# Row moves in two queues, routing in three steps, shared PSUM banks and earlier fetches in a four-layer gated network

## The chip, the cores and the metric

The kernel runs on one core of one Trainium2 chip, in one launch. The metric is the device time of one execution in microseconds (us); the number that counts is the median of several timed runs. One execution of each kernel is also recorded by the hardware profiler, and every duration of a single instruction comes from that record.

The engines are written as the profile writes them: PE is the matrix engine and PEld its weight loads, DVE the vector engine, ACT the scalar engine (activation functions and copies), POOL the GpSimd engine, SP the engine that issues most transfers. Each engine carries out its own instructions in the order in which they stand in its stream and waits for the others by semaphores. So an instruction that waits also holds up all that stand behind it on the same engine.

## What is computed

The input x has 32 sequences of 128 tokens with 128 features. Four layers follow, each with an attention part and a feed-forward part, both added to x through a learned gate tanh(g):

```
x = x + tanh(g_xattn[i]) * xattn_i(layernorm(x), ctx, ...)
x = x + tanh(g_ffn[i])   * ffn_i(layernorm(x))
```

- Layer 0: attention of 16 heads (width 8) to the context with a length mask; then a ternary-weight MLP of width 512.
- Layer 1: attention of 16 heads to the context and to x itself; then a block of its own: causal attention with rotary positions (16 heads of width 4), and a mixture of 8 experts of which each token takes its best 2 (width 256, SiLU gate).
- Layer 2: attention of 8 heads (width 16) to the context with a mask; then LayerNorm and a second mixture, best 2 of 8 experts (width 512, GELU).
- Layer 3: instead of attention a "depool": a decaying scan over the context, picked at boundaries that given lengths set, is added to a projection of x; then a feed-forward part whose weights are rounded to three values and whose activations are rounded to 8 bits per token (scale = 127 / max|x|).

The output is x after the fourth layer.

## The kernel before, in words

**Groups.** The 32 sequences are worked on in 8 groups of 4 (`NG`, `NB`). x stays on chip for the whole run, one tile per group (`xs[g]`).

**Attention.** `attention` cuts a group's heads into units of four and each unit into two halves. For a half it does three things: the maxima of the scores (products L476 on PE, `sc`, reduced by DVE at L507 or L512), which `placed` turns (L526) and writes into the stacked operand as extra rows by a transfer on SP (`mrows`); the weights (products `sct`, L476, then Exp on ACT, L542; L545 on POOL cuts off later tokens in the causal attention); and the products with the values (L559), whose result is copied (L565), turned (L571) and divided by its sum.

**The pipe.** `Pipe` sets the order in which the work is written down. One `turn` takes the maxima of one half, the weights of a half four turns back (`AHEAD`), and the products one turn after that. After each turn it carries out some of the row moves that are waiting (`move`), and one step of the first generator in `afters` (what follows a group's attention) and in `fill` (work put beside it: the MLP of layer 0; in layer 2 `last_layer`, which prepares the depool and the rounded weights of layer 3). `attend` runs it over all groups, the next group's `before` being advanced turn by turn; `drain` finishes what is left. A scheduler then places each engine's instructions; the order of the DMA moves on POOL is kept as written.

**Norms.** `layernorm` takes statistics on DVE (L211, L213) and leaves the power to -1/2 to POOL: `r` (L201), or, where two norms in a row are merged (`again`), `w` (L247); DVE waits for it and then scales (L234).

**Routing.** `Routes.take` gets the logits of a group (`pl`, L1052 in layer 1, L1216 in layer 2), takes softmax and the best two on DVE, and counts each expert's tokens by a product with a triangle (`pos`, L655 and L656), which gives each token a slot (`slot_r`, L662). It then queues 8 stores: each is an indirect DMA issued by POOL (L609) that writes 128 rows into the experts' rooms in DRAM. `Routes.run` goes through 23 blocks of 512 slots: it loads weights and rows (SP, L728 and L730), turns the rows (`transposed`, L265), and applies the expert (L1085 to L1090, or L1233 and L1236), the second product (`ye`, L746), and the way back (`yT`, L1094 or L1240, `yt`, L753). `fetch` then queues 8 indirect reads per group on POOL (L776), and `add` adds them with their weights on DVE (L788).

**The move queue.** Stores and fetches stand in one list, `to_move`. In layers 0 and 1 a turn issues 2 of them, in layer 2 4 of them; layer 2's `before(g)` empties the list before it adds, and queues the next group's fetch when it ends.

**PSUM.** Layer 2 has two accumulators for L559 (`av`), two tiles of two banks for scores, and two banks (`tp`) for all else. The expert loops have two banks for transposes, one for `ye`, four for the first products.

**Layer 3.** `depooled(g)` issues all queued moves, adds, takes the merged norm (w), queues the fetch of group g+1, and adds the projection and the depool, which layer 2 left in eight tiles on chip. `first(g)` takes the norm (r), issues the queued fetch, rounds (`quantized`: maximum L1254, then L1255, L1257, L1258, L1260 and the rounding L1263), and applies the gate and up weights (L1303, L1305, L1308). `second(g, h)` rounds again and applies the last product (L1324). The loop runs `depooled(g+2)`, `first(g+1)`, `second(g)`. The weights of this layer (`w3`) are loaded at L1064.

Of the kernel before, what the change touches and what calls it, by code (L numbers as in the profile page):

```python
# [25 lines left out]
SLOTS = 512  # L26
CAP = 4096
D = 128
EPS = 1e-5
MORE = (2 * CAP - E) // SLOTS  # L30
BLOCKS = E * CAP // SLOTS + MORE + 1
# [3 lines left out]
class _Cols:  # L35
# [15 lines left out]
    iota_p=1, rev=8, room=8,  # L51
# [10 lines left out]
W3 = _Cols(w_in=128, gate=512, up=512, down=512)  # L62


@with_exitstack
def tile_flamingo_gated(
# [316 lines left out]
    to_place, to_finish, to_move = [], [], []  # L383

    def move(n=None):
        for do in to_move[:n]:
            do()
        del to_move[:n]

    class Pipe:  # L390
# [6 lines left out]
        def __init__(self, moves):  # L397
            self.moves = moves
            self.todo, self.last, self.afters, self.place, self.fill = [], None, [], [[]], []

# [16 lines left out]

        def turn(self, ahead):
            self.place.append(to_place[:])
            to_place.clear()  # L420
            place = self.place.pop(0)
            ready = bool(self.afters)
            for do in to_finish + place:
                do()
            to_finish.clear()
            if len(self.todo) > ahead:
                self.todo[0][0]()
            if self.last:
                _, products, after = self.last
                products()  # L430
                if after:
                    self.afters.append(after())
            self.last = self.todo.pop(0) if len(self.todo) > ahead else None
            move(self.moves)
            if ready:
                self.advance(self.afters)
            self.advance(self.fill)

        def drain(self):
# [7 lines left out]
            move()  # L447
            while self.fill:
                self.advance(self.fill)
# [137 lines left out]
    class Routes:  # L587
# [3 lines left out]
        def __init__(self, keep, name):  # L591
            self.name = name
            self.slot = keep.tile([P, NG, 2, NB], I32, name=f"slot_{name}")
            self.weight = keep.tile([P, NG, 2, NB], F32, name=f"weight_{name}")
            self.total = keep.tile([P, E], BF, name=f"total_{name}")
            nc.vector.memset(self.total, 0.0)
            self.room = by_expert.pop()
# [17 lines left out]
        def take(self, pool, psum, g, logits, rows, gate, eps):  # L615

            def t(tag):
# [4 lines left out]

            tt = nc.vector.tensor_tensor
# [29 lines left out]
            tt(self.total, before[:, NB - 1], mine[:, NB - 1], ALU.add)  # L653
            pos = psum.tile([P, NB, E], F32, tag="tp", name="pos")
# [3 lines left out]
            tt(at, pos, CST(cst, "room")[:, None, :].to_broadcast([P, NB, E]), ALU.add)  # L658
# [4 lines left out]
            for b in range(NB):  # L663
                for k in range(2):
                    to_move.append(lambda b=b, k=k: self.store(rows[:, b, :], self.slot[:, g, k, b : b + 1]))
# [8 lines left out]
            )  # L674

        def tables(self, pool, psum):


            n = MORE
# [3 lines left out]
            nc.vector.tensor_scalar(nx, cnt, 1.0 / SLOTS, 0.5 - 0.5 / SLOTS, ALU.mult, ALU.add)  # L683
# [17 lines left out]
            nc.vector.tensor_scalar(row[:, 2], row[:, 0], float(CAP // SLOTS), 1.0, ALU.mult, ALU.add)  # L701
# [6 lines left out]
        def run(self, pool, psum, weights, cols, turned, hidden, n_f, finish):  # L708
# [3 lines left out]
            def static(i):  # L712
                return slice(i * (CAP // SLOTS), i * (CAP // SLOTS) + 1), slice(i, i + 1)

            def dynamic(i):
# [5 lines left out]
                    for k, top in ((1, BLOCKS - 1), (0, E - 1))  # L721
                ]
                return bass.ds(vals[0], 1), bass.ds(vals[1], 1)

            def load(i):
# [3 lines left out]
                xt = pool.tile([P, SLOTS // P, D], F32, tag="xt", name="xt", bufs=3)  # L729
# [5 lines left out]

            def first(i):
                block, w, xt = loaded.pop(i)
                xT = pool.tile([P, SLOTS], F32, tag="xT", name="xT")
                turned(xT, flat(transposed(psum, xt)))
                return block, w, hidden(w, xT)  # L740

            def second(block, w, hid):
                y = psum.tile([P, SLOTS], F32, tag="y", name="ye", bufs=1)
# [3 lines left out]
                yT = pool.tile([P, NB, P], F32, tag="yT", name="yT")  # L747
# [3 lines left out]
            def third(block, yT):  # L751
                yt = pool.tile([P, NB, D], F32, tag="yt", name="yt")
                nc.vector.tensor_copy(yt, transposed(psum, yT))  # L753
                ins = nc.sync.dma_start(out=self.room[block].rearrange("o p n -> (o p) n"), in_=flat(yt))
                self.apart(ins, "tiles", "no two tiles share a block")

            n = E + MORE
            loaded = {0: load(0), 1: load(1)}
            hid, done = first(0), None
            table = self.tables(pool, psum)  # L760
            for i in range(n):
# [6 lines left out]
                hid = after  # L768
            third(*done)

        def fetch(self, pool, g):

            got = pool.tile([P, 2, NB, D], F32, tag="got", name="got")
# [8 lines left out]
            to_move.extend(lambda b=b, k=k: one(b, k) for b in range(NB) for k in range(2))  # L782
            return got

        def add(self, g, got):
            for b in range(NB):
                for k in range(2):
                    nc.vector.scalar_tensor_tensor(  # L788
                        xs[g][:, b, :], got[:, k, b, :], self.weight[:, g, k, b : b + 1], xs[g][:, b, :],
# [14 lines left out]
    def attend(pipe, banks, jobs):  # L804


        layer, g = jobs[0]
        for _ in layer.before(g):
            pass
        for i, (layer, g) in enumerate(jobs):  # L810
            then, n = jobs[i + 1] if i + 1 < len(jobs) else (None, None)
# [4 lines left out]
        pipe.drain()  # L816

# [25 lines left out]

    by_expert = [dram.tile([BLOCKS, P, SLOTS // P * D], F32, name=f"by_expert{i}") for i in range(2)]
    clear = [(t, n) for t in by_expert[::-1] for n in range(0, BLOCKS, 4)]
    routes1 = Routes(cp, "r1")
    with ExitStack() as stack:
# [6 lines left out]
        class psum:  # L854


            @staticmethod
            def tile(shape, dtype, tag=None, name=None, bufs=None):
                return psum_h.tile(shape, dtype, tag="h", name=name)

        pipe = Pipe(2)
# [3 lines left out]
        def layer0():  # L865
# [5 lines left out]
            zeros = mlp.tile([P, SLOTS // P * D], F32, name="zeros")  # L871
            nc.gpsimd.memset(zeros, 0.0)
            def cleared():
                if clear:
                    t, n = clear.pop(0)
                    nc.sync.dma_start(
                        out=t[n : n + 4].rearrange("n p m -> p n m"),
                        in_=zeros[:, None, :].to_broadcast([P, 4, SLOTS // P * D]),
                    )
# [53 lines left out]
            def after(g):  # L933
                add_gated(xs[g], 0, at.pop(g)[-1])
                pipe.fill.append(mlp0(g))
                yield
# [5 lines left out]
        def layer1():  # L942
# [28 lines left out]
            def after(g):  # L971
# [13 lines left out]
                yield  # L985
# [3 lines left out]
        def layer1f():  # L989
# [42 lines left out]
            def after(g):  # L1032
# [20 lines left out]
                routes1.take(pool, psum, g, pl, t, 5, 0.0)  # L1053
                yield
# [10 lines left out]
    depool = [tail.tile([P, NB, D], F32, name=f"depool{g}") for g in range(NG)]  # L1065
# [4 lines left out]
    with ExitStack() as outer:  # L1070
# [3 lines left out]
        with ExitStack() as stack:  # L1074
# [5 lines left out]
            def swiglu(w, xT):  # L1080
                hid = pool.tile([P, 2, SLOTS], F32, tag="hid", name="hid", bufs=3)
                for f in range(2):
                    fs = slice(f * P, (f + 1) * P)
                    p1 = psum.tile([P, SLOTS], F32, tag="h", name="p1", bufs=4)
                    nc.tensor.matmul(p1, lhsT=E1(w, "w1")[:, fs], rhs=xT, start=True, stop=True)  # L1085
                    p3 = psum.tile([P, SLOTS], F32, tag="h", name="p3", bufs=4)
                    nc.tensor.matmul(p3, lhsT=E1(w, "w3")[:, fs], rhs=xT, start=True, stop=True)  # L1087
                    sil = pool.tile([P, SLOTS], F32, tag="sil", name="sil", bufs=3)
# [7 lines left out]
            routes1.run(pool, psum, e1_d, E1, turned, swiglu, 2, finish)  # L1096


        routes2 = Routes(cp, "r2")
        with ExitStack() as stack:  # L1100
            banks = attention_pools(stack, "a2", 2, 4)
            pool, psum, _, _ = banks
            pipe = Pipe(4)
# [3 lines left out]
            def last_layer():  # L1107
# [13 lines left out]
                for g in range(NG):  # L1121
# [43 lines left out]
                    nc.scalar.copy(depool[g], po)  # L1165
# [24 lines left out]
            def before(g):  # L1190
                if g == 0:
                    gots[0] = routes1.fetch(pool, 0)
                move()
# [10 lines left out]
            def after(g):  # L1204
# [14 lines left out]
                routes2.take(pool, psum, g, pl, yn, 6, 1e-8)  # L1219
                yield  # L1220
# [248 lines left out]
```

## Time and profile before

| | us |
|---|---|
| timed runs | 2245.47, 2238.03, 2245.99 |
| median of them | 2245.47 |
| the profiled execution | 2218.45 |
| its span, first to last instruction | 2216.7 |
| layers 0 and 1 with their attention (from the span's start) | 0 to 1250 |
| first expert loop | 1250 to 1420 |
| attention of layer 2 and its routing | 1420 to 1800 |
| second expert loop | 1800 to 2005 |
| layer 3 | 2005 to 2217 |

The profile's page gives for each engine its busy time, share of the span and number of instructions:

```profile
PE 1651.2 (74%) x13624; PEld 1005.0 (45%) x13624; DVE 1219.5 (55%) x3521; ACT 894.8 (40%) x1110; POOL 643.3 (29%) x645
```

In the same page the span is cut into 40 slices of 55.4 us. A digit is the busy share of a slice in tenths, and PEclk is the clock that PE was granted, in tenths of full speed:

```profile
PE   0699998989999998878777399545656449993444
DVE  7645455375545577676666333366677421113777
POOL 5101011010100113345554660254544310004440
PEclk9999999999999999877778599866677569996656
```

PE is nearly full through the first sixteen slices (layers 0 and 1) and again in slices 33 to 37 (the second expert loop). Between them, in layer 2 (slices 26 to 32), and after them, in layer 3, all engines have gaps. A line of a list of waits reads: engine and tile that waited, what it waited for, us in all, how many times, the longest. In a timeline a line is start, duration, engine, line of the code, operation, and in brackets the idle time before it and what ended it.

### The profile page before, as it was taken

Reading aid. Unit: us, or ns where it says so; the run is one execution under the profiler, and the core shown is the slowest. Engines: PE = TensorE matmul, PEld = TensorE weight load, DVE = VectorE, ACT = ScalarE, POOL = GpSimd, SP = SyncE. Lnnn points to the kernel's source line nnn. Section 1 sums busy time; section 2 is a strip of 40 time slices with the busy share of each in tenths; the row PEclk is TensorE's granted clock in tenths of the full one; section 3 lists DMA queues with packets and bytes.
Section 4 is the critical chain, followed back from the end, with each engine's and each line's share of the span. In section 5 each row is a group of like instructions: output and inputs, shape, how many; then the busy total and the mean of one; then the engine's idle time right before and its main releaser. Section 6 shows DMA issues by size and latency. Waiting matters only on the chain.

```text
span 2216.7 us, 35517 instructions
## 1 busy us (share of the span) xinstructions
PE 1651.2 (74%) x13624; PEld 1005.0 (45%) x13624; DVE 1219.5 (55%) x3521; ACT 894.8 (40%) x1110; POOL 643.3 (29%) x645
## 2 busy tenths in 40 slices
PE   0699998989999998878777399545656449993444
PEld 0454445456666666555455144233545324441222
DVE  7645455375545577676666333366677421113777
ACT  0376565556777654332333133211112114341334
POOL 5101011010100113345554660254544310004440
PEclk9999999999999999877778599866677569996656
DMA  6574567544232342112121254244344023331110
GB/s 213 147 244 164 181 204 274 162 116 121 86 99 89 99 118 67 51 54 58 51 60 34 79 167 149 94 115 127 99 119 109 21 84 124 118 116 38 29 36 22
DMA packets 162232, 240.46 MB, mean 108 GB/s; under 512 B 20304, under 2 KB 102032, under 8 KB 161808
## 3 DMA queue, kind: packets, MB, share of 16 engines
q1 hardware_dynamic: 153872, 221.42, 32.6%
q0 software_dynamic: 8192, 16.79, 2.7%
q8 instruction: 107, 1.75, 0.3%
q14 instruction: 61, 0.50, 0.1%
HBM read 137.64 MB, written 99.14 MB: 107 GB/s over the span
## 4 chain that ended last, share of the span: by engine, by line
PE 39%; DVE 14%; POOL 13%; issue 7%; ACT 3%; DMA 3%; SPq 0%; POOLq 0%; DVEq 0%; ACTq 0%
PE ye L746 5%; POOL got L776 5%; PE sct L476 4%; PE av L559 4%; POOL by_expert L609 4%; PE ph L1233 4%; PE sc L476 3%; PE ph L918 3%; PE tp L265 3%; DVE mx L507 2%; DMA got<-by_expert,slot_r 2%; PE p L1087 2%; PE p L1085 2%; DVE bst L211 1%; PE tpo L571 1%
## 5 line engine op out<-in xcount | busy, mean ns | idle before, releaser
L542 ACT ACTIVATE w<-sct 128x1024 f32<-128x1024 f32 x288 | 292.6, 1024 | 315.4 <-PE sct L476 312.8
L507 DVE TENSOR_REDUCE mx<-sc 128x8 f32<-128x1024 f32 x160 | 194.6, 1218 | 133.1 <-PE sc L476 132.5
L476 PEld LDWEIGHTS <-stack_q 96*128 96x128 bf16 x2560 | 189.0, 107 | 119.9 <-issue 96.1
L776 POOL DMA_INDIRECT got<-by_expert,slot_r x128 | 126.5, 989 | 354.9 <-issue 354.1
L559 PE MATMUL av<-w,va 128*9 128x128 f32 (+2 forms) x3584 | 200.4, 296 | 37.8 <-POOL w L545 31.7
L512 DVE TENSOR_REDUCE mx<-sc 128x4 f32<-128x1024 f32 x128 | 152.8, 1221 | 130.0 <-PE sc L476 129.5
L476 PE MATMUL sc<-stack_k,stack_q 96*128 96x128 bf16 x1536 | 141.7, 237 | 40.6 <-DVE mx L507 16.5
L476 PE MATMUL sct<-stack_q,stack_k 128*128 128x128 bf16 (+1 forms) x1536 | 140.0, 234 | 21.8 <-DVE mx L507 12.7
L476 PEld LDWEIGHTS <-stack_k 128*128 128x128 bf16 (+1 forms) x1536 | 109.5, 105 | 76.0 <-issue 72.7
L559 PEld LDWEIGHTS av<-w,va 128*9 128x9 f32 (+2 forms) x3584 | 100.2, 94 | 88.4 <-POOL w L545 42.3
L294 POOL CAST hml<-whole 128x512 bf16<-128x512 f32 (+1 forms) x56 | 36.7, 655 | 354.7 <-ACT whole L293 181.5
L746 PE MATMUL ye<-hid,w 128*128 128x512 f32 x276 | 133.3, 593 | 2.3 <-DVE hid L1090 2.3
L201 POOL TENSOR_TENSOR r<-r,m 128x4 f32<-128x4 f32 x56 | 57.1, 1020 | 230.9 <-DVE r L200 219.7
L918 PE MATMUL ph<-h,w 128*128 128x512 f32 x256 | 122.7, 606 | 1.8 <-ACT hn L921 0.9
L918 PE MATMUL ph<-hn,w 128*128 128x512 f32 x256 | 121.2, 604 | 0.7 <-ACT hn L921 0.7
L565 ACT COPY ot<-av 128x512 f32<-128x512 f32 x112 | 65.4, 584 | 128.9 <-PE av L559 90.7
L476 PE MATMUL sc<-stack_l,stack_q 96*128 96x128 bf16 x1024 | 109.8, 237 | 0.0
L1227 DVE TENSOR_SCALAR xT<-tp,col 128x512 f32<-128x512 f32 x23 | 18.6, 809 | 154.9 <-PE tp L265 137.5
L545 POOL TENSOR_SCALAR_AFFINE_SELECT w<-w 128x1024 f32<-128x1024 f32 x64 | 70.3, 1098 | 109.5 <-ACT w L542 109.4
L476 PE MATMUL sct<-stack_q,stack_l 128*128 128x128 bf16 x1024 | 98.8, 234 | 2.7 <-DVE mx L507 2.5
L542 ACT ACT_TABLE_LOAD x72 | 92.4, 1283 | 9.7 <-PE sct L476 8.5
L571 PE MATMUL tpo<-cst,ot 128*128 128x128 f32 x448 | 81.2, 305 | 13.7 <-ACT ot L565 6.6
(289 smaller groups left out, 3345.2 us busy)
## 6 DMA issues: line engine op xcount, KB each, us to landing
by_expert<-zeros SPq DMA_DIRECT2D x40, 1024.0 KB
stack_q<-q SPq DMA_DIRECT2D x96, 288.0 KB
stack_k<-k SPq DMA_DIRECT2D x96, 288.0 KB
k<-hml SPq DMA_DIRECT2D x16, 1152.0 KB
w<-in_e_dram SPq DMA_DIRECT2D x23, 514.5 KB
xt<-by_expert SPq DMA_DIRECT2D x46, 256.0 KB
by_expert<-yt SPq DMA_DIRECT2D x46, 256.0 KB
q<-hml SPq DMA_DIRECT2D x72, 128.0 KB
```

Of the source, the lines that this page charges most:

```text
L476: nc.tensor.matmul(dst[:, h * P : (h + 1) * P], lhsT=stat[rows, 4 * e + h, b], rhs=mov[rows, 4 * e + h, b], start=start and h == e == 0, s ...
L507: nc.vector.tensor_reduce(mx[:, :, b0 : b0 + 2].rearrange("p h b -> p b h"), sc.rearrange("p i (h k) -> p i h k", h=4), AX.X, ALU.max, neg ...
L512: nc.vector.tensor_reduce(mx[:, :, b0], sc.rearrange("p i (h k) -> p h i k", h=4), AX.XY, ALU.max, negate=True,)
L542: nc.scalar.activation(w.rearrange("p i h k -> p i (h k)"), sc, AF.Exp)
L545: nc.gpsimd.affine_select(out=heads, in_=heads, pattern=[[0, 8], [1, P]], compare_op=ALU.is_ge, fill=0.0, base=0, channel_multiplier=-1,)
L559: nc.tensor.matmul(av[32 * h : 32 * h + dv + 1, b * P : (b + 1) * P], lhsT=values[c][:, b, 4 * u + h, :], rhs=w[:, i, h, :], start=c == 0, ...
L571: nc.tensor.transpose(tp[:, b].rearrange("p s r -> p (s r)"), ot[:, b, :], ident)
L609: ins = nc.gpsimd.indirect_dma_start(out=self.rows(), out_offset=bass.IndirectOffsetOnAxis(ap=slots, axis=0), in_=rows, in_offset=None,)
L746: nc.tensor.matmul(y, lhsT=w2[:, f, :], rhs=hid[:, f, :], start=f == 0, stop=f == n_f - 1)
L776: ins = nc.gpsimd.indirect_dma_start(out=got[:, k, b, :], out_offset=None, in_=self.rows(), in_offset=bass.IndirectOffsetOnAxis(ap=self.sl ...
L918: nc.tensor.matmul(ph, lhsT=wt[:, c, f * P : (f + 1) * P], rhs=h[:, c, :], start=c == 0, stop=c == 3)
L1233: nc.tensor.matmul(ph, lhsT=E2(w, "w1")[:, f * P : (f + 1) * P], rhs=xT, start=True, stop=True)
```

## The change

Eight things are altered.

1. `to_move` becomes two lists. A turn issues up to 3 fetches and 2 stores in every layer. Layer 2's `before(g)` empties only the list of fetches; `drain` issues what is left of the stores after all `afters` are done, and steps the work beside it meanwhile.
2. `Routes.take` yields twice: after the counts on DVE, before `pos`; and after the weights, before it queues the stores. The stores are queued one step later than before.
3. Layer 2's attention has one accumulator, four banks for scores as before, and three banks that all else shares (`shared`).
4. The depool rows go to DRAM by SP and come back, group by group, in layer 3.
5. The expert loops have two banks for `ye` and three for the first products.
6. In layer 3, `fetch(g)` issues the loads of the depool and the 8 fetches at once. `depooled(g)` does this for g+1 and g+2 right after its norm; the fetched rows have three buffers.
7. `quantized` computes max(am, 1e-5)/127 and its reciprocal (before: maximum, reciprocal, times 127, reciprocal), and the two products `fg` become one instruction.
8. The experts' rooms, slots and blocks are computed from a table (`LOTS`), with the values that they had. A few `yield`s at the ends of `after` go.

The load L1064 of layer 3's weights is written at the same place; in the built order it stands far earlier, since the pool that it belongs to has become smaller.

```diff
+        def beside(self):
+            for i, (fill, rate) in enumerate(self.fills):
+                self.owed[i] += rate
+                while self.owed[i] >= 1:
+                    self.owed[i] -= 1
+                    self.advance(fill)
...
-            move(self.moves)
+            move(to_fetch, 3)
+            move(to_store, 2)
             if ready:
                 self.advance(self.afters)
-            self.advance(self.fill)
+            self.beside()
...
-        def drain(self):
+        def flush(self):
             while self.todo or self.last:
                 self.turn(0)
...
             while self.afters:
                 self.advance(self.afters)
-            move()
-            while self.fill:
-                self.advance(self.fill)
+                self.beside()
+
+        def drain(self):
+            self.flush()
+            move(to_store)
+            for fill, _ in self.fills:
+                while fill:
+                    self.advance(fill)
...
             tt(self.total, before[:, NB - 1], mine[:, NB - 1], ALU.add)
+            yield
             pos = psum.tile([P, NB, E], F32, tag="tp", name="pos")
...
-            for b in range(NB):
-                for k in range(2):
-                    to_move.append(lambda b=b, k=k: self.store(rows[:, b, :], self.slot[:, g, k, b : b + 1]))
...
+            yield
+            for b in range(NB):
+                for k in range(2):
+                    to_store.append(lambda b=b, k=k: self.store(rows[:, b, :], self.slot[:, g, k, b : b + 1]))
...
-                y = psum.tile([P, SLOTS], F32, tag="y", name="ye", bufs=1)
+                y = psum.tile([P, self.slots], F32, tag="y", name="ye")
...
+    def shared(pool):
+
+        class psum:
+            @staticmethod
+            def tile(shape, dtype, tag=None, name=None, bufs=None):
+                return pool.tile(shape, dtype, tag="h", name=name)
+
+        return psum
...
-    depool = [tail.tile([P, NB, D], F32, name=f"depool{g}") for g in range(NG)]
+    depool = [dram.tile([P, NB * D], F32, name=f"depool{g}") for g in range(NG)]
...
-                    p1 = psum.tile([P, SLOTS], F32, tag="h", name="p1", bufs=4)
+                    p1 = psum.tile([P, 512], F32, tag="h", name="p1", bufs=3)
...
-            banks = attention_pools(stack, "a2", 2, 4)
-            pool, psum, _, _ = banks
-            pipe = Pipe(4)
+            pool, psum_a, avs, _ = attention_pools(stack, "a2", 1, 4)
+            psum_h = stack.enter_context(tc.tile_pool(name="beside_ps", bufs=3, space=PSUM))
+            psum = shared(psum_h)
...
-                    nc.scalar.copy(depool[g], po)
+                    nc.scalar.copy(dep, po)
+                    nc.sync.dma_start(out=depool[g], in_=flat(dep))
...
-                move()
+                move(to_fetch)
                 routes1.add(g, gots.pop(g))
...
-                    ph = psum.tile([P, SLOTS], F32, tag="h", name="ph", bufs=4)
+                    ph = psum.tile([P, 512], F32, tag="h", name="ph", bufs=3)
...
-            nc.vector.tensor_scalar(am, am, 1e-5, None, ALU.max)
+            inv = pool.tile([P, NB], F32, tag=f"inv_{tag}", name=f"inv_{tag}")
+            nc.vector.tensor_scalar(inv, am, 1e-5, 1.0 / 127.0, ALU.max, ALU.mult)
             sc = pool.tile([P, NB], F32, tag="qs", name="qs")
-            nc.vector.reciprocal(sc, am)
-            nc.vector.tensor_scalar(sc, sc, 127.0, None, ALU.mult)
-            inv = pool.tile([P, NB], F32, tag=f"inv_{tag}", name=f"inv_{tag}")
-            nc.vector.reciprocal(inv, sc)
+            nc.vector.reciprocal(sc, inv)
...
+        def fetch(g):
+            if g < NG and g not in fetched:
+                dp = pool.tile([P, NB, D], F32, tag="dp", name="dp", bufs=3)
+                nc.sync.dma_start(out=flat(dp), in_=depool[g])
+                fetched[g] = routes2.fetch(pool, g, 3), dp
+                move(to_fetch)
+
         def depooled(g):
-            move()
-            routes2.add(g, fetched.pop(g))
+            got, dp = fetched[g]
+            routes2.add(g, got)
             _, h = layernorm(pool, xs[g], tag=None, again="hx")
-            if g + 1 < NG:
-                fetched[g + 1] = routes2.fetch(pool, g + 1)
+            fetch(g + 1)
+            fetch(g + 2)
...
             y = layernorm(pool, xs[g])
-            move()
             q, inv = quantized(y, D, "x")
...
+        fetch(0)
         depooled(0)
         depooled(1)
         h = first(0)
```

## The prediction, made before the changed kernel was run

> **What bounds the kernel now.** I read first the table of windows, one per stage: busy us, then the granted TensorE clock.
>
> ```profile
> 0.00:1250.00 1250.00, 1038.17 (x10218) 642.16 (x10218) 749.59 (x1959) 632.12 (x723) 317.69 (x356) 0.93 0.39 120
> 1250.00:1440.00 190.00, 147.73 (x463) 72.34 (x463) 63.89 (x109) 55.97 (x93) 72.05 (x35) 0.90 0.43 139
> 1440.00:1700.00 260.00, 149.47 (x1517) 116.87 (x1520) 173.27 (x670) 46.77 (x64) 133.33 (x141) 0.67 0.43 113
> 1700.00:1800.00 100.00, 41.11 (x415) 32.46 (x407) 48.84 (x223) 11.92 (x17) 35.97 (x35) 0.59 0.13 40
> 1800.00:2005.00 205.00, 188.51 (x559) 90.28 (x559) 36.56 (x59) 80.18 (x116) 0.00 (x0) 0.97 0.35 119
> 2005.00:2217.00 212.00, 86.26 (x460) 50.85 (x460) 147.38 (x504) 67.85 (x97) 84.22 (x80) 0.62 0.11 30
> ```
>
> The columns are PE, PEld, DVE, ACT, POOL, clock, DMA share, GB/s. Layers 0 and 1 (to 1250) and the two expert loops (to 1440, to 2005) are PE's. In layer 2 (1440 to 1800) and the last layer (from 2005) no engine is full: waits decide. So I read the waits there, then the timelines of DVE and POOL, and last the chain of one period. Layer 2's waits, 1440 to 1700, and the expert loops' (1290 to 1418, then 1810 to 1995):
>
> ```profile
> PE pos L655 <- DVE t_mine L648: 31.6, 4, 12.0
> DVE y L234 <- POOL r L201: 25.3, 8, 7.2
> DVE y L234 <- POOL w L247: 10.2, 5, 5.2
> ```
>
> ```profile
> PE tp L265 <- ACT yT L1094: 6.0, 21, 0.7
> ```
>
> ```profile
> PE tp L265 <- ACT yT L1240: 8.3, 21, 0.4
> ```
>
> PE stands in front of the routing's `pos` product 31.6 us, and DVE for the LayerNorms' powers on POOL 35.5 us. DVE's timeline in the tail of layer 2, the idle time before each in brackets:
>
> ```profile
> 1742.87 0.18 DVE L245 TENSOR_SCALAR w<-bmv 128x4 f32<-128x4 f32 x1
> 1751.12 1.12 DVE L234 TENSOR_SCALAR y<-x,bmv,w 128x128 f32<-128x128 f32 x4 [8.07 <-POOL w L247]
> ...
> 1767.69 0.16 DVE L245 TENSOR_SCALAR w<-bmv 128x4 f32<-128x4 f32 x1
> 1777.05 1.11 DVE L234 TENSOR_SCALAR y<-x,bmv,w 128x128 f32<-128x128 f32 x4 [9.20 <-POOL w L247]
> ```
>
> The power itself takes 1.67; the rest is eight stores (L609) queued ahead of it. The chain of one period of the last layer, 2091 to 2116:
>
> ```profile
> by line: POOL got L776 32.9%; DMA got<-by_expert,slot_r 20.5%; issue 11.7%; PE px L1279 7.3%; PE po L1324 5.5%; DVE bst L211 5.4%; POOL r L201 4.0%; DVE t L1329 2.8%; DVE h L1308 2.7%; PE tph L1319 2.6%; DVE x L273 2.6%; DVE bmv L213 2.3%;
> ...
> 2091.42 2.57 DMA got<-by_expert,slot_r
> ...
> 2103.78 1.01 POOL r L201
> 2104.96 1.01 POOL got L776
> ```
>
> There the chain runs through POOL's fetches and their landing.
>
> **The change part by part.** The base is the profiled execution, 2218.45 us (span 2216.7). A fetch or store holds POOL 0.95 with a 0.30 gap: eight take 10.0. Orders are those of the built changed kernel.
>
> *Causal attention of layer 1 (900 to 1240).* In five groups DVE waits for the first rotary add (L1020), 23.0 us in all: it starts at 1101.42 behind seven stores, inputs ready at 1095.7. Afterwards five stand there (six, then five, in one group): 2 x 1.25 x 5 = -12.5 at most. The two moved stores come later, one before the casts of the next parts. I take half: -6 (-11 to 0).
>
> *Layer 2 to 1700.* Three edits with one answer. Routing in pieces puts up to 27 score products and the transposes ahead of `pos` on PE in the first four groups: at most the 31.6 goes. But DVE (173 of 260 us) must still do each routing and the maxima. Three shared banks let transposes wait less for one another; only one accumulator bank stays, which the copy (L565, 0.58 us) must clear first: near nothing. The two queues put three instead of eight fetches ahead of the second group's stores (-5), but later powers stand behind up to seven stores and four fetches: +3 to +8 each where they are ready early. The depool rows now go to DRAM by SP, each behind an ACT copy; the stack loads behind it in SP's order can start about 3 us later (the first copy ends 1476.56, the next load went at 1473.33). In sum -25 to +20; of 31.6 gained and about 20 lost I take -8, nearer to the wait that is seen.
>
> *Tail of layer 2 (1700 to 1800).* Stores queue after all pieces of the groups, and only three of a group's own stand ahead of the next power instead of eight. Those powers were ready at 1717.1, 1743.05 and 1767.85 and ran at 1720.67, 1749.42 and 1775.34. The first keeps seven stores: -1.3. The second waits for 1739.5 + 3 x 1.25 = 1743.3, say 1743.5: -5.9. The third likewise 1769.3: -6.0. Behind each stands the path to the end: y, transpose, logits, routing, slot. The last group's 13 stores: five find the 11.8 us idle before 1788.77. -13 (-17 to -2; little if PE's or SP's work is late instead).
>
> *Expert loops.* A second bank for the second product lets the transpose of yT stand further from its copy: it waits 6.0 us in 128 and 8.3 us in 185. Over the loops at most -6 and -8. Three instead of four banks for the first products give some back: the fourth reuses a bank that a 0.8 us activation must free. Half: -7 (-14 to +5).
>
> *Weights of the last layer.* Their load (L1064, 0.85 MB) went ahead of the first expert's, whose rows landed 5.49 us after issue; it now goes far earlier: -2 (-3 to 0).
>
> *Last layer.* Now each power r follows w and then eight fetches; before it was w, r, fetches. Start: w0 ends 2020.61, sixteen fetches 20.0, w1 at 2040.8 (was 2033.76), eight fetches, r0 at 2052.7 (was 2037.14): +15.6. Steady: w to r becomes 1.67 + 0.2 + 10.0 = 11.9 (was 7.8, 2095.97 to 2103.78); r to w loses the waits for landing (0.24 + 1.33 + 0.76 = 2.3) and six small quantizer steps of about 0.1: 14.9 - 2.9 = 12.0. A period goes from 22.7 to 23.9: +1.2, four times. The last three groups have no fetch ahead of r and no landing to wait for: -2.3 each. 15.6 + 4.8 - 6.9 = +14 (+5 to +18). So what is late next, once the landings are covered, is the power behind the issue.
>
> One fetch per period ran 1.25 instead of 0.94, starting 2089.87, beside the 1.70 us quantizer (L1263, from 2089.29). [...]
>
> *Start.* Three groups' statistics precede the first y: +1 (-1 to +3), nearest to L211's 0.2 us each.
>
> Sum: -6 - 8 - 13 - 7 - 2 + 14 + 1 = **-21**, 2197.5 on the profiled base. The median of the runs shown is 2245.47, 1.2% above the profile; scaled, 2245.47 x 2197.5/2218.45 = **2224**.
>
> **The rivals.**
> (a) *Attention in layer 2 is set free* (0.2): PE's 31.6 us go nearly whole. For: PE is busy only 149 of 260. Against: DVE's 173. Body -30: sum -43, 2202.
> (b) *The gains are not on the path* (0.2): in the tail SP's row loads for the last groups end later than the power, and the loops stay at PE's rate (62.6 of 65 busy). Tail -4, loops 0, body 0: sum +3, 2249. For: PE waited 1.38 for a row load at 1741.
> (c) *POOL's order takes the place of the waits* (0.15), the other side: powers behind moves, in the body as in the last layer. Four more transfers ahead of each of five powers: 5 x 5 = +25 there, +18 at the end: -6 + 25 - 13 - 7 - 2 + 18 + 1 = +16, 2262. It decides once the body loses over 13, that is 2.6 us a group. For: two power waits, 35.5 us. Against: POOL is busy 133 of 260.
>
> **How the numbers follow.** The forecast has 0.45, spread 2210 to 2240. Half a per cent, 11 us, is about what a measurement can tell. Faster by more: 0.43 of the forecast, all of (a): 0.63. Within: 0.02 and (b): 0.21. Slower: (c) and a spare 0.01: 0.16. The range from 2198 to 2254 takes in the forecast, (b) and most of (a) and leaves out (c).
>
> **What would show it.** The window 1700 to 1800 ends some 13 us shorter, with DVE's wait for w (L247) under 3 us; `pos` waits shrink before 1700; the transposes of yT no longer wait; and from the end of the second loop to the end it takes 226 instead of 212, with r behind eight fetches and no wait of DVE for landings. It is wrong if the last layer does not lengthen, or if powers in layer 2's body wait over 50 us.

## The result, and the profile after

The changed kernel took 2214.01 us (median of four runs, 2206.13 to 2221.30), the kernel before 2241.75 beside it (four runs): a ratio of 0.988, 95% interval 0.983 to 0.993, forecast 0.990 (2224). Two repeats gave 0.9907 (0.9884 to 0.9930) and 0.9892 (0.9878 to 0.9907).

Yet its profiled execution is the longer one: span 2219.6, against 2216.7 in the table above. Chips differ by more than that. On the chip of the first series of runs below, the kernel before took 2240 (23 runs) and its own profiled execution 2238; on that of the second series it took 2218 (23 runs). The profile shown ahead of the prediction is like the second. So stages are compared here between traces of one series wherever there are such.

The windows of the changed kernel, cut at its own stages, columns as before:

```profile
1264.00:1424.00 160.00, 147.77 (x463) 69.76 (x463) 54.54 (x87) 56.10 (x93) 55.86 (x17) 0.96 0.47 148
1424.00:1700.00 276.00, 154.77 (x1394) 118.15 (x1394) 167.59 (x651) 42.41 (x59) 138.06 (x147) 0.63 0.40 114
1700.00:1805.00 105.00, 52.45 (x530) 40.17 (x530) 60.03 (x262) 15.96 (x22) 44.91 (x44) 0.65 0.17 53
1805.00:2003.00 198.00, 185.51 (x555) 87.67 (x555) 36.57 (x59) 80.11 (x116) 0.95 (x1) 0.97 0.36 123
2003.00:2219.00 216.00, 81.28 (x458) 49.32 (x464) 139.53 (x464) 67.95 (x97) 83.86 (x80) 0.63 0.14 39
```

Both expert loops are shorter with nearly the same PE work (147.8 and 185.5 us busy, against 147.7 and 188.5): 160 and 198 us. The last layer is longer, 216, although DVE has less to do there (139.5 against 147.4). Now DVE's timeline in the tail of layer 2:

```profile
1759.66 0.25 DVE L252 TENSOR_SCALAR w<-bmv 128x4 f32<-128x4 f32 x1
1764.18 1.28 DVE L241 TENSOR_SCALAR y<-x,bmv,w 128x128 f32<-128x128 f32 x4 [4.27 <-POOL w L254]
1780.06 0.24 DVE L252 TENSOR_SCALAR w<-bmv 128x4 f32<-128x4 f32 x1
1784.58 1.28 DVE L241 TENSOR_SCALAR y<-x,bmv,w 128x128 f32<-128x128 f32 x4 [4.27 <-POOL w L254]
```

The lines are those shown of before (L241 and L254 were L234 and L247): the idle time fell from 8.07 and 9.20 to 4.27 each, since three stores, not eight, stand ahead of the power. POOL's timeline at the start of the last layer:

```profile
2037.91 1.67 POOL L254 TENSOR_TENSOR w<-w,m 128x8 f32<-128x8 f32 x1
...
2048.71 0.95 POOL L821 DMA_INDIRECT got<-by_expert_r,slot_r  x1 [0.30 <-issue]
2049.66 1.05 POOL L208 TENSOR_TENSOR r<-r,m 128x4 f32<-128x4 f32 x1
```

r0 runs 46.3 us after the first fetch, where it ran after 31.1: it stands behind eight fetches, which it does not need.

The table gives each stage in the first series, one chip for both; "slots" are the times at which DVE writes a group's slots.

| stage | before | changed | difference | forecast |
|---|---|---|---|---|
| start to the first group's slots | 945.3 | 949.4 | +4.1 | +1 |
| causal attention: first to eighth slots | 298.0 | 297.8 | -0.2 | -6 |
| first loop: landing of the last store to first fetch | 167.6 | 159.8 | -7.8 | -2 and part of -7 |
| body of layer 2: first fetch to fifth slots | 304.1 | 304.7 | +0.6 | -8 |
| tail of layer 2: fifth to eighth slots | 82.6 | 69.2 | -13.4 | -13 |
| second loop: issue of the last store to first fetch | 208.4 | 199.0 | -9.4 | part of -7 |
| last layer | 208.7 | 216.9 | +8.2 | +14 |
| span | 2236.4 | 2218.5 | -17.9 | -21 |

### The profile page after: what moved, and what is told of

Read it like the earlier page. It is cut to its first block, busy times and chain, and to the rows that moved or that the text cites. A ratio compares the mean times of both kernels' runs of the same rounds, so it can differ in the third digit from the quotient of the medians.

```text
span 2219.6 us, 35462 instructions
## 1 busy us (share of the span) xinstructions
PE 1666.0 (75%) x13618; PEld 1010.1 (46%) x13624; DVE 1205.2 (54%) x3480; ACT 894.5 (40%) x1110; POOL 648.9 (29%) x645
## 4 chain that ended last, share of the span: by engine, by line
PE 40%; DVE 14%; POOL 13%; issue 5%; DMA 3%; ACT 2%; another core or an unknown queue 2%; SPq 0%; POOLq 0%; DVEq 0%; ACTq 0%
PE ye L786 5%; PE av L581 4%; PE sct L498 4%; PE ph L1294 4%; PE ph L969 4%; POOL got L821 4%; PE sc L498 3%; POOL by_expert_r L636 3%; PE p L1135 2%; PE tpe L773 2%; PE p L1137 2%; POOL w L254 1%; PE tp L272 1%; DVE mx L529 1%
## 5 line engine op out<-in xcount | busy, mean ns | idle before, releaser
L498 PEld LDWEIGHTS <-stack_q 96*128 96x128 bf16 x2560 | 194.6, 109 | 130.7 <-issue 100.4
L581 PE MATMUL av<-w,va 128*9 128x128 f32 (+2 forms) x3584 | 207.6, 298 | 41.9 <-POOL w L567 26.5
L821 POOL DMA_INDIRECT got<-by_expert_r,slot_r x128 | 126.6, 989 | 336.8 <-issue 335.9
L498 PE MATMUL sc<-stack_k,stack_q 96*128 96x128 bf16 x1536 | 148.6, 245 | 47.1 <-DMA stack_k<-k 16.9
L498 PE MATMUL sct<-stack_q,stack_k 128*128 128x128 bf16 (+1 forms) x1536 | 145.3, 239 | 22.7 <-DVE mx L529 13.7
L498 PEld LDWEIGHTS <-stack_k 128*128 128x128 bf16 (+1 forms) x1536 | 114.1, 108 | 78.7 <-issue 75.3
L1294 PE MATMUL ph<-xT,w 128*128 128x512 f32 x184 | 86.6, 613 | 0.8 <-DVE nx L714 0.8
```

Source lines behind the costliest of these rows:

```text
L498: nc.tensor.matmul(dst[:, h * P : (h + 1) * P], lhsT=stat[rows, 4 * e + h, b], rhs=mov[rows, 4 * e + h, b], start=start and h == e == 0, s ...
L581: nc.tensor.matmul(av[32 * h : 32 * h + dv + 1, b * P : (b + 1) * P], lhsT=values[c][:, b, 4 * u + h, :], rhs=w[:, i, h, :], start=c == 0, ...
L821: ins = nc.gpsimd.indirect_dma_start(out=got[:, k, b, :], out_offset=None, in_=self.rows(), in_offset=bass.IndirectOffsetOnAxis(ap=self.sl ...
L1294: nc.tensor.matmul(ph, lhsT=E2(w, "w1")[:, f * P : (f + 1) * P], rhs=xT, start=True, stop=True)
```

## The experiments

There are three series of four kernels, each on one chip. The ratio is always to the kernel before in the same series, which took 2240, 2218 and 2235 us. The first series has the next four kernels (both again, the fetches as before, the banks as before); the second has routing in one step, layer 2's PSUM, the depool store and the parted fetches on the changed kernel; the third has the rest. The changed kernel itself was not run in the second, so there the kernels that leave a stage as changed stand for it.

### Both kernels again, for traces of one chip

No edit.

> The kernel before, unchanged, run beside the changed one on one chip, for its trace. Theory A (the gain of 1.2% is real, and the profiled execution of before that was shown, 2218.45 us, was an uncommonly quick one): ratio 1.000 within 0.4%, and its trace is 20 to 30 us longer than that one, the surplus spread over stages whose code the change leaves alone (layers 0 and 1). Rival B (the profiled execution is typical, and the timed gain comes from the chip): trace of 2215 to 2222 us here too, no longer than that of the changed kernel.

> The changed kernel on the same chip. Theory A: ratio 0.988 (0.983 to 0.993); by stage against the trace of before on this chip: both expert loops shorter by 7 to 11 us each, tail of layer 2 (fifth to eighth group's slots) shorter by 10 to 13, body of layer 2 (first fetch to the fifth group's slots) longer by 0 to 17, last layer longer by 3 to 8. Rival B: ratio 0.998 to 1.004, with the same differences by stage.

The kernel before: 2237.56, ratio 0.9995 (0.9979 to 1.0010), span 2236.4. The changed one: 2218.26, ratio 0.9907 (0.9884 to 0.9930). Theory A holds: the timed gain is real, and the first profile was a quick one. But its surplus on this chip does not lie in layers 0 and 1, as A said: they end within 2 us of it. It lies in the body (304.1 against 288.4) and the tail (82.6 against 78.0) of layer 2. The loops and the tail came as expected; the last layer lost 8.2, where 3 to 8 was expected.

### The last layer's fetches as before

```diff
                 fetched[g] = routes2.fetch(pool, g, 3), dp
-                move(to_fetch)
...
+            move(to_fetch)
             got, dp = fetched[g]
...
             fetch(g + 1)
-            fetch(g + 2)
...
             y = layernorm(pool, xs[g])
+            move(to_fetch)
```

> The changed kernel with the fetches of the last layer issued as before: one group ahead, after the power r instead of ahead of it. The rest of the change stays. Theory A (powers behind the issue of fetches): last layer 5 to 6 us shorter than in the changed kernel, start (first fetch to r0) 31 instead of 46 us; ratio to before about 0.985. Rival B (what lengthens the last layer is the depool rows from DRAM or DVE's order, not POOL's): last layer within 2 us of the changed kernel's 216, although r0 comes 15 us sooner.

2209.81, ratio 0.9854 (0.9828 to 0.9879). The last layer took 205.0, 11.9 less than in the changed kernel beside it, and r0 came after 30.6 us, not 46.2. Theory A's cause holds and its size was too small: the new order costs 12. The 3.7 by which 205.0 lies under the 208.7 of before is what the rest of the last layer's edits gives, the short quantizers among them.

### The banks of the expert loops as before

```diff
-                y = psum.tile([P, self.slots], F32, tag="y", name="ye")
+                y = psum.tile([P, self.slots], F32, tag="y", name="ye", bufs=1)
...
-                    p1 = psum.tile([P, 512], F32, tag="h", name="p1", bufs=3)
+                    p1 = psum.tile([P, 512], F32, tag="h", name="p1", bufs=4)
```

(and likewise for p3 and ph)

> The changed kernel with the PSUM of the expert loops as before: one bank for the second product, four for the first. Theory A (the second bank frees the transposes behind their copies): both loops together 16 to 19 us longer than in the changed kernel, ratio to before about 0.996. Rival B (the loops gain by the earlier weight load or by the other rows' layout, not by the banks): loops within 4 us of the changed kernel's.

2233.67, ratio 0.9962 (0.9940 to 0.9984). The loops took 164.0 and 209.1, together 14.3 more than in the changed kernel: the banks carry most of it, a little less than expected. The first loop stays 3.6 under before's 167.6. Of this, 2.6 lies at its start: the first transpose on PE comes 6.4 us after the last store has landed in the kernel before, and 3.8 here, where the load of the last layer's weights no longer goes first. No run moved this load alone.

### Only the banks of the loops, on the kernel before

The same edit the other way round, on the kernel before (third series).

> The kernel before with only the banks of the expert loops changed (two for the second product, three for the first). Theory A: both loops together 14 us shorter (163 to 165 and 198 to 199, against 167.6 and 208.4), ratio 0.993 to 0.995. Rival B (the loops need the earlier weight load and the new rows as well): 8 us or less.

2225.33, ratio 0.9951 (0.9939 to 0.9964). The loops took 162.8 and 198.1: 15.1 less than 167.6 and 208.4. Theory A; the banks need no other edit. The timed gain is only 10; the causal attention, whose code is the same, took 299.4 in this kernel's trace against 294.2 in that of the parted fetches in the same series. Stretches of 90 us in the middle of the second loop show how the banks work, the kernel before first, then the changed one (first series):

```profile
1850.00:1940.00 90.00, 85.64 (x261) 41.53 (x260) 16.52 (x22) 37.66 (x55) 0.00 (x0) 1.00 0.36 123
```

```profile
1830.00:1920.00 90.00, 90.00 (x274) 42.81 (x273) 17.21 (x23) 38.49 (x57) 0.00 (x0) 1.00 0.37 126
```

PE went from 85.64 busy with 261 products to all 90 with 274, at the same granted clock (1.00 in both). The 4.4 us that PE stood idle are all gone. PE's waits for yT in both loops, the kernel before and then the changed one (first series):

```profile
PE tp L265 <- ACT yT L1240: 10.0, 23, 0.8
PE tp L265 <- ACT yT L1094: 6.4, 23, 0.7
```

```profile
PE tpe L773 <- ACT yT L1301: 0.8, 1, 0.8
PE tpe L773 <- ACT yT L1144: 0.7, 1, 0.7
```

They fell from 16.4 us to 1.5, which is what the banks are worth within a microsecond.

### Routing in one step

```diff
-            yield
             pos = psum.tile([P, NB, E], F32, tag="tp", name="pos")
...
-            yield
             for b in range(NB):
```

> The changed kernel with the routing written in one step again, its stores queued at once (the two queues stay). Seven or eight of a group's own stores then stand ahead of the next power in the tail of layer 2, as in the kernel before, instead of three. Theory A (the later stores make the tail shorter): the slots of the fifth to eighth group span 76 to 83 us instead of 67 to 69; ratio to before about 0.995. Rival B (the tail is shorter because of the shared PSUM banks or the two queues): tail 65 to 70 us here too, ratio within 0.002 of the changed kernel's 0.9907.

2210.74, ratio 0.9974 (0.9957 to 0.9991), on the second chip. The tail took 71.0, against 64.2 in the two kernels of this series that leave layer 2's order as changed or nearly so. That is 6.8 of some 14 (the first profile of before has 78.0), and neither theory had it. The expectation counted seven or eight stores ahead of the power in the tail; in the built order six stood there for the last two groups, where before has eight and the changed kernel three. DVE's waits for these two powers lie between as well, 6.58 each, against 8.07 and 9.20 before and 4.27 changed:

```profile
1754.12 1.28 DVE L241 TENSOR_SCALAR y<-x,bmv,w 128x128 f32<-128x128 f32 x4 [6.58 <-POOL w L254]
```

So the run puts three of the five stores back, and half of the gain went; what makes the rest was not taken apart. The body is no different (297.2 against 297.7), although PE waits longer for `pos` there; the lists of waits of the body, routing in one step and then the changed order (the kernel with the parted fetches):

```profile
PE pos L684 <- DVE t_mine L677: 38.2, 5, 13.8
```

```profile
PE pos L685 <- DVE t_mine L677: 19.5, 5, 4.9
```

So these waits were no price of the path. What no theory had: the causal attention took 294.9 instead of 282.1. More of it below.

### Layer 2's PSUM as before

```diff
-            pool, psum_a, avs, _ = attention_pools(stack, "a2", 1, 4)
+            banks = attention_pools(stack, "a2", 2, 4)
+            pool, psum, _, _ = banks
```

(the shared pool and `apart` are left out)

> The changed kernel with layer 2's PSUM as before: two accumulators, four banks for scores, two for all else. Theory A (the banks are worth next to nothing): body 300 to 309 us, tail 65 to 71, ratio within 0.002 of the changed kernel's 0.9907. Rival B (three shared banks carry the gain of layer 2): body or tail longer by 5 us or more, ratio 0.993 or over.

2208.83, ratio 0.9959 (0.9941 to 0.9978). Body 302.0 and tail 67.4, against 297.7 and 64.2: the shared banks are worth about 4 and 3 us here, once each, less than B's 5. The ratio says more than that, but 8.7 of its us lie in the causal attention (290.8 against 282.1), where PE's order is the same in both kernels. In the tail, five stores stood ahead of one power instead of three (DVE waited 6.14 for it instead of 4.27), so its 3 us may come from the built order and not from the banks. Body and tail lie in A's ranges, the ratio in B's: inconclusive as a price.

### The depool store on ACT's queue

```diff
-                    nc.sync.dma_start(out=depool[g], in_=flat(dep))
+                    nc.scalar.dma_start(out=depool[g], in_=flat(dep))
```

> The changed kernel with the depool rows stored from ACT's queue instead of SP's, so that no stack load stands behind a store that waits for ACT's copy (31 us of such waits in SP's stream, in six times). Theory A (those waits hold back the stacks and cost the body what the routing in pieces gains there): body 5 to 15 us shorter than 305, ratio 0.985 to 0.988. Rival B (SP has time to spare; the waits end before the loads behind them are needed): body within 4 us, ratio within 0.002 of 0.9907.

2197.38, ratio 0.9926 (0.9904 to 0.9947). Body 297.4, tail 64.2. The kernel with SP's store in the same series (the next experiment) has 297.7 and 64.2. Rival B: SP's 31 us of waits for ACT's copy held back nothing that was needed.

### The last layer's fetches parted around r

```diff
                 fetched[g] = routes2.fetch(pool, g, 3), dp
-                move(to_fetch)
...
             fetch(g + 1)
-            fetch(g + 2)
+            if g == 0:
+                move(to_fetch)
+            if g > 0:
+                fetch(g + 2)
+            if g > 1:
+                move(to_fetch, 4)
...
             y = layernorm(pool, xs[g])
+            move(to_fetch, 4 if g else 12)
...
         fetch(0)
+        move(to_fetch)
         depooled(0)
```

> The changed kernel with the last layer's fetches parted: four of a group's eight between the power w and the power r, four after r, one and a half groups ahead; the first two groups one at a time, as before. Four take 5.0 us, and r is ready 7.8 us after w started, so that r is not held up and the landings are covered. Theory A: last layer 195 to 203 us (217 in the changed kernel, 205 with the old order), ratio 0.981 to 0.985. Rival B (landings cost little once the quantizers are shorter; DVE's own work sets the period): 203 to 207 us, as with the old order.

2168.15, ratio 0.9795 (0.9769 to 0.9821). The last layer took 188.4, less than theory A's 195: 28 under the changed order, 17 under the old one (205.0 in the first series). The period from w to w fell to 18.5 us.

### Only the parted fetches, on the kernel before

The same edit on the kernel before, with three buffers for the fetched rows (third series).

> The kernel before with only the fetches of the last layer parted around r, one and a half groups ahead, in three buffers; depool on chip and long quantizers stay. Theory A (the order of POOL's queue is what counts): last layer 190 to 194 us instead of 209 to 211, ratio 0.990 to 0.993. Rival B (the gain needs the short quantizers or the depool in DRAM): last layer 200 or more.

2227.26, ratio 0.9965 (0.9950 to 0.9980); last layer 201.3. A's 190 to 194 was missed, B's 200 is reached. In the same series the kernel before with only the loops' banks changed, whose last layer is that of before, took 211.0 there: alone the order gives 9.7 (7.4 against the 208.7 of the first series). Windows of 90 us of the last layer, before with the parted fetches, then the changed kernel with them:

```profile
2060.00:2150.00 90.00, 37.53 (x204) 22.08 (x205) 71.29 (x261) 31.82 (x47) 50.01 (x48) 0.65 0.14 39
```

```profile
2020.00:2110.00 90.00, 41.00 (x248) 24.09 (x248) 80.00 (x274) 34.70 (x51) 51.05 (x49) 0.67 0.17 47
```

With both, DVE is busy 80 of 90 and seems to set the period; with the order alone it still stands idle a fifth. Which of the other edits (quantizers, buffers of the depool, DVE's placement) closes that gap was not taken apart.

### Changed kernel once more, and both good edits together

The second is the changed kernel with the parted fetches and the store on ACT's queue.

> The changed kernel once more, beside the other three. Theory A (the four runs before this one share its tail, loops and layers 0 and 1, and were quicker only by their edits and by the clock granted on their chip): ratio 0.988 to 0.994, last layer 216 to 217, tail 64 to 70, loops 159 and 198. Rival B (the depool store by ACT was worth nothing): on a chip where the kernel before takes about 2218, ratio 0.991 to 0.993, like that of the kernel with the store by ACT (0.9926).

> The changed kernel with both edits that helped or might: fetches of the last layer parted around r, depool rows stored from ACT's queue. Theory A (apart from one another in time, so that they add up): as the parted fetches alone, ratio 0.976 to 0.981, last layer 188. Rival B (the store by ACT costs on ACT what it saves on SP): ratio within 0.001 of the parted fetches alone, 0.9795, or above.

The changed kernel: 2212.06, ratio 0.9892 (0.9878 to 0.9907), last layer 217.3, tail 68.0, loops 159.7 and 199.4. Both edits: 2174.19, ratio 0.9728 (0.9711 to 0.9745), last layer 189.7. This is the best version, 38 us under the changed kernel. The changed kernel came as theory A said, with the last layer and the second loop just over; its rival needed a quick chip, which this was not. The ratio of both edits lies below A's range and so outside B's too. It lies under that of the parted fetches alone (0.9795), but that was another chip; its body (299.2 against 304.7) and tail (63.3 against 68.0) are shorter than the changed kernel's in the same series, which on this chip may be the store's doing and on the second was not. That is left open.

## Why the prediction was right, and where it was not

It forecast 2224 in 2198 to 2254 and faster; 2214 was measured. By the stages of the first series (-17.9 for -21) the total came this near partly by luck. Loops and weights gave 17.2 where 9 were counted, and the last layer lost 5.8 less; against this, body and causal attention gave nothing of their 14, and the start cost 3 more.

- *Tail of layer 2, -13:* -13.4, by the mechanism named: the last two powers stand behind three stores. Between the slots of groups five, six, seven and eight it won 1.3, 5.6 and 6.4, where 1.3, 5.9 and 6.0 had been worked out (the first agrees by chance: in this series that power is held up in neither kernel). DVE's waits for w were to fall under 3 us and are 4.27: their input is now ready earlier, but the three stores start only with the slots, and the power runs 3.9 us after these (10.3 before). The -13 had counted that. With six stores ahead, half of the gain went (routing in one step).
- *Last layer, +14:* +8.2. The start was right (r0 +15.2 where 15.6 was worked out), and undoing the order brought r0 back. The term that was mis-sized is the rest: from r0 to the last r, periods and last groups together were to win 2, and won 6.5. The first four periods took 91.5 instead of 90.1 (+1.4, where +4.8 was counted), the last three 46.3 instead of 54.3 (-8.0 for -6.9). DVE's waits for landings halved (33.6 to 17.2 us), where none was to be left, and its waits for r rose from 4.5 to 22.7. That the power r would be what is late next was right: DVE had its input ready at 2084.75, and it ran at 2093.67. The chain of one period of the changed kernel, 2080 to 2105, shows it:

```profile
2081.12 1.64 POOL w L254
2082.93 1.01 POOL got L821
...
2092.71 0.94 POOL got L821
2093.67 1.06 POOL r L208
```

  The parted fetches showed how far this order is from what the layer can do: 188.
- *Expert loops, -7:* the banks gave -14.3 when they were undone and -15.1 alone. The step that failed is "half": nearly all of PE's waits for yT went (16.4 to 1.5), and nothing shows that three first banks gave any back. The rows for the whole (6 and 8 us) were in the prediction as its bound.
- *Weights of the last layer, -2:* about -2.6 at the start of the first loop, and 1.0 more in it that no run takes apart.
- *Body of layer 2, -8:* +0.6. The step that failed is that PE's wait for `pos` could be turned into time. In the first series' body (to the fifth slots) the wait fell from 33.9 us (22.3, and 11.6 listed under another routing tile, `t_d`) to 21.1, and the body did not get shorter; writing the routing in one step again doubled the wait and changed the body by 0.5. In the second series the body was 9 us above the 288.4 of the first profile, which is one trace of another series; whether the two queues cost something on a quick chip was not tried.
- *Causal attention, -6:* -0.2 in the first series, but 282 us on the second chip against 294.1 in the first profile, and 294.9 with the routing in one step. The first seven groups gained some (-4.5 in the first series: 276.1 to 271.6 from the first to the seventh slots), and the last one lost it again (21.9 to 26.2; 21.7 with one step, so the pieces do it). The granted clock differs as well, 0.77 in the changed kernel of the first series and 0.85 in that with the parted fetches on the second chip (950 to 1100, below); the forecast had no such term.
- *Rivals:* (c)'s mechanism, powers behind moves, is real in the last layer; in the first series the body shows no loss, and DVE's waits for powers there fell from 39.7 to 29.7 us. (a) and (b) did not come: the body gave nothing, and the loops and the tail were on the path.
- *Fetches beside DVE's work.* The 1.70 us that the prediction took for one quantizer instruction is a row of four, of about 0.47 each. Five fetches of the last layer took 1.24 to 1.28 in the first profile of before, the one beside this row among them. The time over 0.95 us of the last layer's 64 fetches adds up to 1.8 in the changed kernel and 2.2 in the kernel before, so the last layer is not longer by it. The longest fetch took 1.90, beside seven adds of DVE of 0.33 each that ran one behind the other; what it waited for was not tried.

## What to carry to other kernels

In this kernel the queue that moves rows on POOL is also that of the norms' powers: r, with its input ready at 2084.75, ran at 2093.67, behind eight fetches. Before issuing more ahead, look at which short instruction stands behind the moves and who waits for it; parting the moves around it took 28 us off a stage of 217. An idle wait of an engine that is not the bound (here PE's 31.6 us for `pos`) is no gain until something on the path ends earlier by it: in the first series it fell from 33.9 to 21.1, and the body did not get shorter. In the loops, where PE was full but for small waits (85.64 of 90 us), they counted whole: 14.9 us of them went, and the banks gave 14.3 and 15.1.

## What the runs showed of the hardware that was not expected

**The same products at two clocks.** In the causal attention the eight products of L1089 took 2.07 us in one group of the changed kernel of the first series; in the same group on the second chip they took 1.16. The windows from 950 to 1100, changed kernel of the first series, then that with parted fetches:

```profile
950.00:1100.00 150.00, 124.90 (x1111) 78.80 (x1110) 101.99 (x327) 47.93 (x65) 85.21 (x85) 0.77 0.21 56
```

```profile
950.00:1100.00 150.00, 119.63 (x1157) 75.51 (x1154) 107.60 (x340) 49.30 (x68) 89.36 (x87) 0.85 0.22 59
```

At a granted clock of 0.85 a group took 44.4 us and the 150 us held 1157 products; at 0.77 it took up to 47.7 and they held 1111. The code of this stage is the same, and so is the order of PE's instructions. These clocks are means; around the products themselves it is 0.5 in the one kernel and 1.0 in the other. The first window below holds the 2.07 us (from 1063.94), the second the 1.16 us (from 1064.10):

```profile
1059.00:1068.00 9.00, 8.27 (x61) 5.56 (x54) 5.67 (x15) 2.40 (x4) 3.12 (x5) 0.50 0.37 83
```

```profile
1063.00:1073.00 10.00, 7.06 (x99) 4.86 (x98) 7.98 (x29) 3.93 (x6) 3.69 (x4) 1.00 0.50 117
```

The chip alone does not decide it: the kernel with layer 2's old PSUM, on the second chip, moved between the two from group to group (44.7 to 47.7). From the first to the eighth slots the causal attention took 297.8 us in the changed kernel of the first series, and on the second chip 290.8 with that old PSUM and 282.1 with the parted fetches. What sets the granted clock was not shown; no run was aimed at it.

**Waits that the profile can't explain.** On the chip of the first series ACT waited for products that PE had ended long before, with no releaser in the trace ("remote"). The same instruction in the kernel before, in the first profile and in the first series:

```profile
1553.40 1.02 ACT L542 ACTIVATE w<-sct 128x1024 f32<-128x1024 f32 x1 [2.28 <-PE sct L476]
```

```profile
1569.27 1.02 ACT L542 ACTIVATE w<-sct 128x1024 f32<-128x1024 f32 x1 [13.93 <-remote]
```

Both kernels have such waits in layer 2 on that chip (ACT before L542 27.5 us in three, and before the same line of the changed kernel 22.6 in three). So has every trace of the third series and the changed kernel's first profile (22 to 38 us); neither the first profile of before nor any trace of the second series has one there. They go with the 16 us by which the body of the kernel before differs between its first profile and the first series. What releases them stays open; no edit was aimed at them.
